# A four-layer convolution and attention kernel: layer 0's middle tap from a moved copy, a rewritten entrance to the attention, and a rewritten end

## The chip, the core and the metric

The kernel runs on one core of one Trainium2 chip. The metric is the time of one execution in device microseconds (us); the runs of the kernel before gave 946.99 to 947.26 us, with a median of 947.2 us. A profiler's record of one execution gives the durations in this document. Its engines are PE (matrix products; PEld is its loading of weights), DVE (the vector engine), ACT (the scalar engine, which evaluates functions), POOL (the general-purpose engine, which also issues some DMAs) and SP (which here only issues DMAs). Each engine works through its own instructions in the order in which they were written to its queue, and waits on semaphores for the others. SBUF is the working memory of 128 partitions; PSUM holds the results of PE in banks of 512 words.

## The reference

Sixteen images of 256 channels and 28 x 28 pixels pass through four layers. Cut to what matters here:

```python
# layer 0: binary activation and binary 3x3 convolution, batch norm over all images, residual
y  = sat_conv2d(sign(x), sign(w0)) * scaling
x  = (y - mean(y)) * rsqrt(var(y) + eps) * gamma + beta + x
# layer 1: sign(x) into a 3x3 convolution with real weights, gates, a 1x1 convolution, batch norms
# layer 2: two binary 3x3 convolutions with batch norm and prelu
out = prelu(binconv(sign(bn(x)), w1), a1)
out = prelu(binconv(sign(bn(out)), w2), a2)
x   = prelu(bn(out) + x, a3)
# layer 3: attention inside each image, N = 784 pixels, 64 channels for q, k and v
q, k, v = Wq @ xf, Wk @ xf, Wv @ xf
attn = softmax(q.T @ k / 8)
x    = Wp @ (attn @ v) + xf
```

A batch norm needs the moments over all sixteen images, so each layer with one ends in a seam: the last image's convolution must be finished before the next layer's first image can be signed.

## The kernel before

The program has a usual form and a careful form; a flag computed on the chip at the end says whether the usual form's result stands. Only the usual form is of interest here. `forward` does layers 0 to 2, `attend_unshifted` the attention, and `leave` its last part, just ahead of the branch on the flag.

**Binary convolutions.** `sign_layer` (line 384) serves layer 0 and both convolutions of layer 2. For each image, `sign_image` has ACT write the signs as 16-bit values into `fpads`, a padded image of 30 x 30 per channel block, two images deep; the products (line 404) read windows of it at column offsets 0, 1 and 2, the three taps of a row. An image of 28 rows takes 36 products of 392 columns. In layer 2, from the image `direct` on, SP also copies the padded image, moved by one element, into `shifted`, and the middle tap reads offset 0 of the copy: its products come after those of the outer taps. Layer 0 has no such copy. After the products ACT takes the upper of two packed results from PSUM (line 420), DVE the lower (line 422), and DVE computes statistics (line 686 in layer 0, 1276 in layer 2). In layer 0 the weights of later layers are prepared beside this, by `steps`: DVE lines 329, 581, 596 and the helper at line 141, which most two-operand steps share. POOL stores each image's integers to `n0d` (line 688). PSUM pairs for the convolutions are three deep.

The order of the instructions on PE, ACT, DVE and SP is written out by hand; that of POOL in layers 0 to 2 is a scheduler's, and in the attention it is by hand too.

**Fillers.** `keep_busy(n)` puts n products on an idle tile into PE's queue, each of 512 columns. One stands near the end of layer 1 (14 products, ahead of the gate's small products), one at the end of layer 2 (35 products, line 506), one in the attention's entrance (8, line 1479).

**The seam into the attention.** `norm("l2c", ..., late=True)` turns the moments into a scale `sg3` (`l2c_r` in the profile) and a shift `bg3` (`l2c_shift`): ACT's square root (line 147), small DVE steps to line 157, then ACT's shift (line 264). For image 0, in halves of 392 pixels, the block k = 1 of the channels gets scale and residual on DVE (line 1642) and the shift on ACT (line 1646); the block k = 0 gets scale and shift on ACT (line 1464) and the residual on DVE (line 1647); then DVE's prelu (line 1649) and the products for queries and keys (`queries_keys`, line 1486). Both halves of the latter hold queries in partitions 0 to 63 and keys in 64 to 127 of the same PSUM bank; three copies, `keys_to` (line 1497) on ACT, `queries` (line 1493) on ACT and `keys_to` on DVE, take them out one after another. An activation at line 1651 loads ACT's table for the exponential ahead of its first use.

**The attention's loop.** Per image: seven chunks of `scores` (line 1509, PSUM tiles "sc", two deep) with ACT's exponential (line 1513); sums of the exponentials in `sum_up`, three on POOL and three on DVE (lines 1521 and 1523), joined in `sum_all` (line 1526); `values` (line 1530), seven chunks into one PSUM bank "av"; `denominators`; the reciprocal (line 1564); the normalizing product (line 1568); and `project` (line 1598, PSUM tile "mi", one deep) with its addition to the image (line 1609). `take_values` (line 1545) is ACT's copy of the values out of PSUM, which `normalize` multiplies. The next image's queries, keys and values (`project_v`, line 1580, `turn_v`, line 1590) stand in between. Images from 2 on are prepared by `finish_a`, where ACT scales and shifts and POOL issues a DMA that adds the residual, and `finish_b`, DVE's prelu (line 1473). In the first turn, image 1 is prepared the same way, with the residual added by DVE (line 1472).

**The end.** For image 15, `doubts_so_far` (five small DVE steps, lines 1618 to 1622) stands between an addition and the reciprocal of image 14. `leave` takes the last denominators by pixel halves, four chunks of values, the flag, the normalization and projection by pixel halves, and three stores on ACT's queue: block 1 in two pixel halves, block 0 whole between them. `usually` is read into a register of every engine, on which each branches after its last instruction.

Of the kernel before, what the change touches and what calls it, by code (L numbers as in the profile page):

```python
# [27 lines left out]
F32 = mybir.dt.float32  # L28
# [62 lines left out]
def forward(ctx: ExitStack, tc: tile.TileContext, d: dict, out: bass.AP, careful: bool):  # L91
# [52 lines left out]
    def rsqrt(name, v, half=None, beside=None):  # L144

        r, t = (const.tile(list(v.shape), F32, name=name + q) for q in ("_r", "_t"))
        A.activation(t, v, AF.Sqrt)
        if beside:
            beside()
# [88 lines left out]
    def norm(name, moments, gamma, beta, sf=None, then=lambda r: None, late=False):  # L238
# [15 lines left out]
        r = rsqrt(name, v, half, (lambda: V.tensor_scalar(less, m, -1.0, None, ALU.mult)) if late else None)  # L254
# [129 lines left out]
    def sign_layer(pads, w, temp, room, sign, post, steps, moments, blocks, together=1, shifted=None, direct=2):  # L384
# [9 lines left out]
        def products(*js):  # L394
            for j in js:
                pss[j] = conv_ps()
            moved = shifted is not None and blocks[js[0]][0] >= direct
# [30 lines left out]
        def sign_image(i):  # L428

            for r0, r1 in ((0, HR + 1), (HR + 1, S)) if i == 0 else ((0, S),):  # L430
                load = sign(i, slice(r0, r1), lambda k: inner(pads[:, i % 2], k, r0, r1))
                if shifted is not None and i >= direct:
                    to, of = (t[:, i % 2].rearrange("p k a b -> p (k a b)") for t in (shifted, pads))
                    nc.sync.dma_start(out=to[:, 0:-1], in_=of[:, 1:])
# [59 lines left out]
    with tc.tile_pool(name="ps_conv", bufs=3, space=PSUM) as psc, \  # L494
# [13 lines left out]
        with tc.tile_pool(name="ph1", bufs=1) as ph:  # L508

            fpads = sign_pads(ph, "vs") if careful else sign_pads(const, None)  # L510
            xs, ns = [None] * B, [None] * B
# [180 lines left out]
            sign_layer(fpads, w0, temp, room0, sign0, post0, steps, mom, whole_images(PARTS), together=2 if careful else 1)  # L692
# [425 lines left out]
            with tc.manual_schedule(engines={ET.PE, ET.DVE, ET.Activation, ET.SP}):  # L1118
# [60 lines left out]
                keep_busy(14)  # L1179
# [33 lines left out]
        with tc.tile_pool(name="ph2", bufs=1) as ph:  # L1213
# [123 lines left out]
            else:  # L1337
                keep_busy(35)
                with tc.manual_schedule(engines={ET.DVE, ET.Activation}):
                    sg3, shift3 = norm("l2c", mom, pv("g3"), pv("b3"), sf2, late=True)  # L1340
                    bg3 = shift3(b3c)
# [78 lines left out]
def attend_unshifted(ctx, tc, d, out, wqk, wv, wp, keys, worst, doubts, flag, pv, finish):  # L1420
# [62 lines left out]
    def queries_keys(b, h, ps):  # L1483

        for k in range(2):
            T.matmul(  # L1486
                ps[:, h, :HN], lhsT=wqk[:, k, :], rhs=x[b][:, k, h * HN:(h + 1) * HN], start=(k == 0), stop=(k == 1)
            )
# [6 lines left out]
    def keys_to(b, rows, h, ps):  # L1495
        copy = A.copy if rows else V.tensor_copy
# [37 lines left out]
    def values(b, c):  # L1534
        if c == 0:
            avs[b] = one_bank(psav, "av")
        side_by_side(avs[b], va[b % 2][:, c, :], es[b, c], c == 0, c == NC_ - 1)
# [98 lines left out]
    with tc.manual_schedule(engines={ET.PE, ET.Activation, ET.DVE, ET.Pool, ET.SP}):  # L1636
# [3 lines left out]
        for n in cuts:  # L1640
            v = x[0][:, 1, n]
            V.scalar_tensor_tensor(v, v, sg3[:, 1:2], x2[0][:, 1, n], ALU.mult, ALU.add)
        for h, n in enumerate(cuts):
            finish_a(0, n, (0,))
            v, w = (x[0][:, k, n] for k in range(2))
            A.activation(w, w, AF.Identity, bias=bg3[:, 1:2])
            V.tensor_tensor(v, v, x2[0][:, 0, n], ALU.add)
            for k, y in enumerate((v, w)):
                V.scalar_tensor_tensor(y, y, alpha[:, k:k + 1], y, ALU.mult, ALU.max)
            queries_keys(0, h, ps[h])  # L1650
        A.activation(ph.tile([P, 2], F32, name="e"), sg3, AF.Exp, scale=0.0)
        keep_busy(8)
        for h in range(2):
            keys_to(0, 1, h, ps[h])
            queries(0, h, ps[h])
            keys_to(0, 0, h, ps[h])
        finish_a(1)
        scores(0, 0)
        project_v(0)
        finish_b(1, ks=(0,))  # L1660
        turn_v(0)
        finish_b(1, ks=(1,))
        V.transpose(ones.rearrange("p a i -> p (a i)"), turned.rearrange("p a i -> p (a i)"))
        for b in range(B - 1):
            scores(b, 1)
            if b > 0:
                take_values(b - 1)
            if b == 0:
                finish_a(2)
            if b > 1:  # L1670
                project(b - 2, 0)()
            sum_up(b, 1)
            scores(b, 2)
# [286 lines left out]
```

## Time and profile before

| what | value |
|---|---|
| median of three runs | 947.2 us |
| the profiled execution's own time | 948.88 us |
| its span, from the first instruction to the last | 947.1 us |
| PE busy | 930.2 us (98%) |
| DVE, ACT, POOL busy | 759.9, 676.1, 139.0 us |
| granted PE clock, mean | 0.996 |
| layer 0 | about 10 to 109 us |
| layer 1 | about 115 to 464 us |
| layer 2 | 464 to 662 us |
| attention | 662 to 940 us, stores and closing to 947 us |

The profile has several views. The chain of waits follows the work that ended last back to the beginning: at each step to what released it, or to the instruction before it on its engine. A piece of it has a start, a length, an engine and the written tile with its line; neighbouring pieces of the same kind are merged with a count. The timeline lists the instructions with start, length, engine, line, operation and tiles, again merged, and in brackets the idle time before. A product in four bytes per word (f32) shows as two records. An engine's busy share is an average over stages with different limits, so each stage is read by itself.

### The profile page before, as it was taken

Reading aid. Unit: us, or ns where it says so; the run is one execution under the profiler, and the core shown is the slowest. Engines: PE = TensorE matmul, PEld = TensorE weight load, DVE = VectorE, ACT = ScalarE, POOL = GpSimd, SP = SyncE. Lnnn points to the kernel's source line nnn. Section 1 sums busy time; section 2 is a strip of 40 time slices with the busy share of each in tenths; the row PEclk is TensorE's granted clock in tenths of the full one; section 3 lists DMA queues with packets and bytes.
Section 4 is the critical chain, followed back from the end, with each engine's and each line's share of the span. In section 5 each row is a group of like instructions: output and inputs, shape, how many; then the busy total and the mean of one; then the engine's idle time right before and its main releaser. Section 6 shows DMA issues by size and latency. Waiting matters only on the chain.

```text
span 947.1 us, 15041 instructions
## 1 busy us (share of the span) xinstructions
PE 930.2 (98%) x5626; PEld 583.6 (62%) x5632; DVE 759.9 (80%) x1446; ACT 676.1 (71%) x1184; POOL 139.0 (15%) x158
## 2 busy tenths in 40 slices
PE   7999999999999999999999999999999999999996
PEld 3555578888788888887555565556444444444442
DVE  3877888999998889987888887889656868777676
ACT  5766578888888788874777767776766666676653
POOL 2001100000000000000000000000235353443422
PEclk9999999999999999999999999999999999999999
DMA  9877533454543344320566201111142433425212
GB/s 334 292 284 272 187 121 122 173 186 177 198 163 139 139 157 163 143 112 35 207 241 214 113 40 60 79 79 59 31 73 70 97 108 81 125 69 136 69 63 112
DMA packets 39733, 130.70 MB, mean 138 GB/s; under 512 B 4882, under 2 KB 16852, under 8 KB 39652
## 3 DMA queue, kind: packets, MB, share of 16 engines
q1 hardware_dynamic: 33332, 98.31, 28.8%
q0 software_dynamic: 5632, 30.54, 11.8%
q8 instruction: 46, 0.75, 0.3%
q10 hardware_dynamic: 688, 0.80, 0.2%
q14 instruction: 35, 0.29, 0.1%
HBM read 72.67 MB, written 32.11 MB: 111 GB/s over the span
## 4 chain that ended last, share of the span: by engine, by line
PE 95%; DVE 2%; ACT 1%; DMA 1%; issue 0%; SPq 0%; DVEq 0%; ACTq 0%
PE cv L404 31%; PE cv L810 29%; PE sc L1509 8%; PE av L1530 8%; PE cv L937 5%; PE mi L1486 5%; PE sm L1580 2%; PE unused L506 2%; PE mi L1598 2%; PE sm L1530 1%; PE gate L905 1%; DMA st<-in_w_dram 1%; PE hid L713 1%; DVE r L1564 1%; DVE p L1609 0%
## 5 line engine op out<-in xcount | busy, mean ns | idle before, releaser
L810 PE MATMUL cv<-vs,w 128*128 128x392 f32 (+1 forms) x1296 | 272.4, 352 | 0.3 <-DVE vs L141 0.3
L404 PE MATMUL cv<-fpads,wpk 128*128 128x392 f16 (+1 forms) x1458 | 249.3, 327 | 2.2 <-DVE wpk L329 1.2
L404 PEld LDWEIGHTS <-wpk 128*128 128x128 f16 x1782 | 172.1, 97 | 123.6 <-issue 4.3
L810 PEld LDWEIGHTS cv<-vs,w 128*128 128x128 f32 x768 | 143.2, 190 | 6.3
L1513 ACT ACTIVATE es<-sc 128x784 f32<-128x784 f32 x112 | 87.4, 823 | 40.0 <-PE sc L1509 40.0
L810 PEld LDWEIGHTS <-w 128*128 128x128 f16 x768 | 69.4, 99 | 51.9 <-issue 9.1
L1509 PE MATMUL sc<-q,keyswa 64*128 64x392 f32 x448 | 89.9, 513 | 1.2 <-ACT es L1513 0.9
L1530 PE MATMUL av<-es,v 128*64 128x392 f32 x448 | 80.7, 499 | 0.0
L1268 DVE SCALAR_TENSOR_TENSOR p<-ab,vec 128x392 f32<-128x392 int16 (+1 forms) x132 | 78.1, 605 | 0.0
L420 ACT ACTIVATE ab<-cv 128x392 int16<-128x392 f32 (+1 forms) x66 | 32.1, 486 | 56.1 <-PE cv L404 53.2
L1523 POOL TENSOR_TENSOR sum<-sum,es 128x784 f32<-128x784 f32 x32 | 67.2, 2101 | 2.5
L1509 PEld LDWEIGHTS sc<-q,keyswa 64*128 64x128 f32 x448 | 38.9, 186 | 44.0 <-issue 17.1
L404 PE MATMUL cv<-shifted,wpk 128*128 128x392 f16 (+1 forms) x324 | 60.6, 322 | 0.0
L810 PE MATMUL cv<-one_on,w 128*128 128x392 bf16 x240 | 59.4, 329 | 0.0
L965 POOL DMA_DIRECT2D x2d<-x x16 | 8.6, 536 | 345.3 <-DVE x L959 285.0
L1497 DVE COPY keyswa<-mi 64x392 f32<-64x392 f32 x31 | 16.3, 564 | 53.2 <-ACT q L1493 53.2
L1530 PEld LDWEIGHTS av<-es,v 128*64 128x64 f32 x448 | 29.4, 136 | 47.0 <-issue 46.6
L422 DVE SCALAR_TENSOR_TENSOR ab<-ab,cv 128x392 int16<-128x392 int16 (+1 forms) x66 | 36.1, 547 | 27.5 <-ACT ab L420 26.6
L792 ACT CAST vs<-vs 128x840 fp32r<-128x840 bf16 x63 | 54.1, 883 | 2.5 <-DVE vs L141 2.3
L937 PE MATMUL cv<-z,fw 128*128 128x392 f32 x256 | 48.9, 342 | 0.1
L937 PEld LDWEIGHTS cv<-z,fw 128*128 128x128 f32 x256 | 46.1, 188 | 0.9 <-ACT z L929 0.9
L1486 PE MATMUL mi<-p,wqk 128*128 128x392 f32 x124 | 45.1, 506 | 0.1
(325 smaller groups left out, 1532.9 us busy)
## 6 DMA issues: line engine op xcount, KB each, us to landing
xs<-in_x_dram SPq DMA_DIRECT2D x30, 784.0 KB, 5.0
one_on<-vs SPq DMA_DIRECT2D x60, 209.8 KB, 2.9
x2d<-x POOLq DMA_DIRECT2D x16, 784.0 KB, 3.6
out_dram<-p SPq DMA_DIRECT2D x15, 784.0 KB, 3.6
shifted<-fpads SPq DMA_DIRECT2D x26, 449.8 KB, 2.8
p<-x2d POOLq DMA_DIRECT2D x14, 784.0 KB, 6.8
p<-x2d SPq DMA_DIRECT2D x13, 784.0 KB, 5.8
n0d<-n POOLq DMA_DIRECT2D x16, 392.0 KB, 4.4
```

What stands on the lines that cost most here:

```text
L404: T.matmul(pss[j][:, n // size if careful else h, :rows * S].rearrange("p (a b) -> p a b", b=S), lhsT=w[:, n, c, :], rhs=src[:, blocks[j][ ...
L420: A.activation(by_halves(ab[:, 1], blocks[j]), ps, AF.Copy, scale=1.0 / PACK)
L422: V.scalar_tensor_tensor(a, b, -PACK, ps, ALU.mult, ALU.add)
L792: copy(v, w)
L810: T.matmul(ps.rearrange("p (a b) -> p a b", b=S), lhsT=w[:, k, c, u, mo * P:(mo + 1) * P], rhs=one_on[:, u, k, :, 0:S] if moved and c == 1 ...
L937: T.matmul(ps[:, h, :HN], lhsT=w[:, k, mo * P:(mo + 1) * P], rhs=z2[b][:, k, h * HN:(h + 1) * HN], start=(k + i == 0), stop=(k + i == 2),)
L1268: V.scalar_tensor_tensor(p, y, alpha[:, mo:mo + 1], y, ALU.mult, ALU.max, accum_out=mom.sums_at(at, mo)[0] if mom.by_sums(at, mo) else None,)
L1486: T.matmul(ps[:, h, :HN], lhsT=wqk[:, k, :], rhs=x[b][:, k, h * HN:(h + 1) * HN], start=(k == 0), stop=(k == 1))
L1509: T.matmul(ps[:, h, :HN], lhsT=chunk[rows], rhs=qs[b][rows], start=True, stop=True)
L1513: A.activation(e, ps[:, :, :HN], AF.Exp, scale=0.125)
L1523: (V if late else nc.gpsimd).tensor_tensor(sums[b, late], sums[b, late], e, ALU.add)
L1530: T.matmul(ps[64 * h:64 * h + 64, :HN], lhsT=w, rhs=e[:, h, :], start=start, stop=stop)
```

## The change

- `sign_layer` gets `until` and `copy`: for images from `direct` up to `until` it makes a moved copy by the given engine. Layer 0 calls it with a tile `moved0`, `until=12` and POOL's `tensor_copy`, so images 2 to 11 read the middle tap from a copy that POOL makes.
- Two fillers are shorter: 14 to 12 in layer 1's end, 35 to 31 before the attention; the one of 8 in the entrance is gone.
- `norm` and `rsqrt` get an activation that loads a table right behind the square root; for `l2c` it is the exponential's. The one in the entrance is gone.
- The entrance is rewritten: both blocks of image 0's first half take scale and residual in one DVE step; the first half's product starts with k = 1; the second half's queries and keys go to two PSUM tiles (`queries_keys_apart`), and both key copies of it are DVE's. `project_v(0)` and `turn_v(0)` come ahead of the first scores. Image 1's second block takes scale and residual on DVE too. Scores 0 to 3, POOL's three sums and values 0 and 1 of image 0 come ahead of image 1's queries and keys, and `finish_a(2)` comes after them.
- `doubts_so_far` moves from image 15 to the loop's turn b = 3.
- Image 14 is normalized from PSUM: no `take_values`, the product reads `av`.
- In `leave`, values run by pixel halves, five chunks each (two chunks stand ahead, not three); the PSUM tiles of the last two projections are swapped; and four stores, one for each block and pixel half, alternate between ACT's queue and SP's.

The diff, without the lines that only shift arguments:

```diff
@@ rsqrt
         A.activation(t, v, AF.Sqrt)
+        if then:
+            A.activation(small.tile(list(v.shape), F32, tag="mv", name="table"), v, then, scale=0.0)
@@ sign_layer
-            moved = shifted is not None and blocks[js[0]][0] >= direct
+            moved = shifted is not None and direct <= blocks[js[0]][0] < until
...
-                if shifted is not None and i >= direct:
+                if shifted is not None and direct <= i < until:
                     to, of = (t[:, i % 2].rearrange("p k a b -> p (k a b)") for t in (shifted, pads))
-                    nc.sync.dma_start(out=to[:, 0:-1], in_=of[:, 1:])
+                    copy(out=to[:, 0:-1], in_=of[:, 1:])
@@ layer 0
+            moved0 = None if careful else ph.tile([P, 2, 2, S + 2, S + 2], SIGNS, tag="vs", name="moved0")
...
-            sign_layer(fpads, w0, temp, room0, sign0, post0, steps, mom, whole_images(PARTS), together=2 if careful else 1)
+            sign_layer(fpads, w0, temp, room0, sign0, post0, steps, mom, whole_images(PARTS), together=2 if careful else 1,
+                       shifted=moved0, until=12, copy=nc.gpsimd.tensor_copy)
@@ layer 1's end
-                keep_busy(14)
+                keep_busy(12)
@@ layer 2's end
-                keep_busy(35)
+                keep_busy(31)
                 with tc.manual_schedule(engines={ET.DVE, ET.Activation}):
-                    sg3, shift3 = norm("l2c", mom, pv("g3"), pv("b3"), sf2, late=True)
+                    sg3, shift3 = norm("l2c", mom, pv("g3"), pv("b3"), sf2, late=True, table=AF.Exp)
@@ attention
+    def queries_keys_apart(b, h, qps, kps):
         for k in range(2):
+            for i, ps in enumerate((qps, kps)):
+                rows = slice(64 * i, 64 * i + 64)
+                T.matmul(
+                    ps[rows, h, :HN], lhsT=wqk[:, k, rows], rhs=x[b][:, k, h * HN:(h + 1) * HN],
+                    start=(k == 0), stop=(k == 1),
+                )
...
-    def values(b, c):
+    def values(b, c, n=slice(0, HN)):
@@ entrance, new
+        for k, n in ((1, one), (0, one), (1, two)):
+            to_x2(0, k, n)
+        for k in (1, 0):
+            shifted(0, k, one)
+            prelu(0, k, one)
+        queries_keys(0, 0, ps[0], (1, 0))
+        finish_a(0, two, (0,))
+        shifted(0, 1, two)
+        add_x2(0, 0, two)
+        for k in range(2):
+            prelu(0, k, two)
+        kps = two_banks(pssc, "sc")
+        queries_keys_apart(0, 1, ps[1], kps)
+        keys_to(0, 1, 0, ps[0])
+        queries(0, 0, ps[0])
+        keys_to(0, 0, 0, ps[0], A.copy)
+        queries(0, 1, ps[1])
+        for rows in range(2):
+            keys_to(0, rows, 1, kps, V.tensor_copy)
+        finish_a(1, ks=(0,))
+        to_x2(1, 1)
+        project_v(0)
+        turn_v(0)
         scores(0, 0)
+        scores(0, 1)
+        shifted(1, 1)
+        add_x2(1, 0)
+        for k in range(2):
+            prelu(1, k)
+        sum_up(0, 1)
+        scores(0, 2)
+        scores(0, 3)
+        sum_up(0, 2, 3)
+        for c in range(2):
+            values(0, c)
+        finish_a(2)
@@ loop
             if b > 0:
                 denominators(b - 1)
+                if b == 3:
+                    doubts_so_far()
                 invert(b - 1)
@@ image 15
-        take_values(b - 1)
+        os[b - 1] = (buf("o", 2, shape=(P, HN)), buf("r", 2, shape=(P, HN)))
...
-        doubts_so_far()
...
-        normalize(b - 1)
+        o, r = os[b - 1]
+        V.tensor_tensor(o, avs[b - 1][:, :HN], r, ALU.mult)
...
-        for c in range(3):
+        for c in range(2):
             values(b, c)
@@ leave
-            for c in range(3, NC_):
-                values(b, c)
+            for n in parts:
+                for c in range(2, NC_):
+                    values(b, c, n)
...
-                adds.append(project(b, mo, two_banks(pssc, "sc") if mo else two_banks(psmi, "mi"), parts[1]))
+                adds.append(project(b, mo, two_banks(psmi, "mi") if mo else two_banks(pssc, "sc"), parts[1]))
...
-            nc.scalar.dma_start(out=by_parts[0], in_=by_parts[1])
-            store(b, slice(0, 1), nc.scalar)
-            nc.scalar.dma_start(out=by_parts[2], in_=by_parts[3])
+            for n in parts:
+                for mo, queue in enumerate((nc.scalar, nc.sync)):
+                    to, of = (halves(t[:, mo, :])[:, :, n] for t in (out[b], x[b]))
+                    queue.dma_start(out=to, in_=of)
```

## The prediction

> **What bounds the kernel now.** I read the page first, then the chain of waits in order of time, then the timeline around each place that the diff touches. The page says that the chain is TensorE nearly throughout, at full granted clock:
>
> ```profile
> PE 95%; DVE 2%; ACT 1%; DMA 1%; issue 0%; SPq 0%; DVEq 0%; ACTq 0%
> ```
>
> So a change pays only where it shortens PE's stream or a seam between stages. The chain's pieces (start, length, what) show both:
>
> ```profile
> 10.46 98.73 PE cv L404 x588
> ...
> 566.25 96.11 PE cv L404 x594
> 662.41 7.51 PE unused L506 x34
> 670.02 1.55 PE mi L1486 x4
> ...
> 674.84 0.93 PE sc L1509 x4
> ...
> 925.02 2.53 DVE r L1564
> ...
> 927.64 1.47 DVE o L1568
> ...
> 934.28 2.66 PE av L1530 x16
> ```
>
> Layer 0 needs 98.73/588 = 167.9 ns per product; layer 2's second convolution, which reads its middle tap from a moved copy, 96.11/594 = 161.8 ns. The starts within one image say why: products of the middle tap follow after 177 ns, the others after 165 to 170. A whole image lasts 6.12 us in layer 0 and 2 x 2.985 = 5.97 us in layer 2. From 662 to 675 the seam is filler, a wait for copies, then attention; from 916 DVE leads.
>
> DVE and POOL exclude each other, as the timelines show (start, length, engine, line):
>
> ```profile
> 743.13 2.05 DVE L1523 TENSOR_TENSOR sum<-sum,es 128x784 f32<-128x784 f32 x1
> ...
> 750.67 0.93 DVE L1521 TENSOR_TENSOR sum<-es 128x784 f32<-128x784 f32 x1
> ...
> 924.89 3.78 POOL L1523 TENSOR_TENSOR sum<-sum,es 128x784 f32<-128x784 f32 x2
> ...
> 927.64 1.46 DVE L1568 TENSOR_TENSOR o<-o,r 128x392 f32<-128x392 f32 x1
> ```
>
> The same addition takes 0.93 alone and 2.05 beside a POOL addition; the product o<-o,r takes 0.57 in other images and 1.46 here. L1609, which adds PSUM to SBUF, keeps 0.97 either way.
>
> **Layer 0's moved copies.** Images 2 to 11: 12 middle-tap products of 36 each get cheaper, 6.12 - 5.98 = 0.14 us per image, **-1.4 us**. The copy of 1799 halfwords runs on POOL. No row shows one: POOL's fill of 448 words took 0.47 (1.05 ns per element, hence 1.9 us), its addition of 784 with two inputs 1.85 (2.36 ns, hence 4.25 us). I take 1.9, since a copy has one input. The copy starts when ACT's signs end, 2.4 us after the preceding image's products begin, and is wanted 6.0 + 24 x 0.166 = 10.0 us after that: 7.6 us of room. POOL's queue also issues n0d (0.54), after DVE's L422; both ends fit in 6.0 us together. Who waits for POOL is DVE's weight work (two SBUF inputs: L141, L596, L329), which follows the statistics at about 3.9 us into the image, so 0.4 us of waiting at 1.9 us per copy. DVE is busy 3.4 to 5.4 us of 6.1 per image there, and three PSUM pairs let L422 lag; hidden. [...] at 4.25 us per copy DVE would wait 2.8 us per image, and still recover between copies. Images 12 to 15 and layer 0's end keep their times.
>
> **Fillers in layer 1's end (14 to 12).** The filler ends at 459.43; the gate's sums are ready at 458.91, but ACT is in its square until 459.50, so ACT's hidden unit moves from 459.79 to 459.52. The square root after the table load also needs DVE's variance (462.15), so it moves from 462.34 to 462.19: **-0.15** (0 to -0.3).
>
> **The attention's entrance.** Exp's table now loads behind the root, at 666.36, before the shifts that ACT began at 667.24. They begin at 667.76, and the first half's entry is shifted at 668.96, not 668.51. Before, the load cost nothing:
>
> ```profile
> 670.02 1.55 PE L1486 MATMUL mi<-p,wqk 128*128 128x392 f32 x4
> 670.16 1.28 ACT L1651 ACT_TABLE_LOAD   x1
> ...
> 671.45 0.20 ACT L1651 ACTIVATE e<-l2c_r 128x2 f32<-128x2 f32 x1
> ...
> 671.67 0.48 ACT L1497 COPY keyswa<-mi 64x392 f32<-64x392 f32 x1
> ```
>
> It ended with PE's products. [...] here the next activation starts at 1.29, so I charge 1.3[...]. Onward with these rows (0.58 per half-image DVE step, 0.51 to 0.61 on ACT): DVE does three entries by 668.97, prelu k=1 at 669.58, k=0 at 670.14. The filler (31 x 0.215) ends at 669.1, no longer in the way; PE's k=1 product starts at 669.65, the half is done at 671.15 (before 671.57). Second half: ACT 670.07 and 670.59, DVE's last prelu 671.81, PE done at 672.83 (673.10). Queries and keys now lie in two PSUM tiles: one ACT copy beside two DVE copies, not three in turn; keys complete at 673.9, while PE does project_v until 674.2. Scores 0 and 1 start there and end by 675.9; before, the same work ended at 678.1. Then ACT's exponentials gate PE: scores 2 and 3 end at 677.5, values 0 and 1 at 678.9.
>
> Next late is image 1's last prelu (L1473, two SBUF inputs). POOL's sums are new here: the first, ready at 676.85, waits for DVE's first prelu (676.5 to 677.5), [...] and the second prelu, ready at 677.6, ends at 680.25. PE's image-1 keys end at 682.4, not 681.8; pv, scores 4 to 6, the remaining values and image 1's first scores (all by their old rows) end at 690.4, against 692.18: **-1.8** (-2.4 without the block; +0.5 if POOL takes two turns). On POOL's queue image 2's accumulating load now stands behind three sums: issued at 684, not 681.1, landing 6.6 later at 690.7; its two prelus end at 692.7 and PE wants them at 693.2 and 693.9. Small cover: later sums go straight onto the path.
>
> **doubts_so_far, moved to b = 3.** Five small DVE steps, 0.95 us from the tail's row. In the steady loop nothing covers them:
>
> ```profile
> 753.52 2.61 DVE L1564 RECIPROCAL r<-sm 128x392 f32<-128x392 f32 x1
> ...
> 756.16 0.57 DVE L1568 TENSOR_TENSOR o<-o,r 128x392 f32<-128x392 f32 x1
> ...
> 756.65 0.97 DVE L1609 TENSOR_TENSOR p<-mi,p 128x784 f32<-128x784 f32 x1
> ...
> 757.76 0.84 PE L1598 MATMUL mi<-o,wp 64*128 64x392 f32 x4
> ```
>
> L1609 frees the only "mi" buffer at 757.62 and PE takes it at 757.76: 0.1 of slack, so **+0.85** once.
>
> **The tail.** Without the doubts the reciprocal of image 14 starts when the denominators are there, 924.2 (925.0 before). Normalizing from PSUM escapes POOL: 0.57, done at 927.4 (929.1), and ACT's copy goes. PE then waits for score banks (ACT until 928.5): projections 928.15 to 929.5, two values to 930.9, then DVE's last sum, ready 931.3 (POOL holds it until 928.7). Denominators end at 932.95 (the bank must be freed at 932.25), against 934.28. Values by pixel halves: 40 records of 196 columns at 0.083 (L1558's 8 took 0.66), end 936.3 against 936.94, the first half at 934.6. DVE's reciprocals end at 935.8, o's at 936.75, and with the two PSUM tiles swapped only the fourth addition waits: the last ends at 939.05, not 940.34: -1.3.
>
> The stores: same bytes, four of 784-byte rows. Before, the last was issued at 940.37, landed at 945.37, and 1.7 us of closing followed[...]. Now the last issue is near 939.1, moving done by 941.0, landing 941.6 to 943.2. But SP branches only after its last store: the trace has 2.5 us from SP's branch to its next instruction, 4.2 for ACT and DVE. SP resumes at 942.1 to 943.8, passes nine semaphores (0.7), then 1.65 of closing: the span ends at 944.4 to 946.1, not 947.1: **-1.0 to -2.7, taken -1.8**.
>
> **Sum.** -1.4 - 0.15 - 1.8 + 0.85 - 1.8 = -4.3. The profiled execution took 948.88 (span 947.1 and 1.8 around it) and would take 944.6; the runs' median is 947.2 and would be **943.0**.
>
> **Rivals.**
> - *The entrance is eaten by POOL's sums*: [...] image 2's load lands after 693. For it: the rows above[...]. Entrance +0.3 instead of -1.8: 945.1.
> - *POOL bounds layer 0 (slower)*: if a copy costs X, each image costs X + 0.54 instead of 6.12. From X = 5.9 us on it outweighs all other gains (2.9); at 7 us it is 10 x 1.42 = +14.2, so 958.5. Against: the two-input row gives only 4.25.
> - *The middle tap doesn't follow the copy* (layer 2 differs in something else): no 1.4, 944.4. The start-to-start times speak against.
> - *The tail gives more*: [...] entrance unblocked: 941.3.
>
> **Chances.** Forecast 0.58 (own range 941.8 to 944.4), entrance eaten 0.17, no tap gain 0.08, better tail 0.10, POOL-bound 0.07. A measurement tells 0.2% (1.9 us, so 945.3 and 949.1). Faster takes all but the slow rival and some of the eaten entrance: 0.80; same 0.12; slower 0.08. The range leaves out the slow rival and a little at each end: 940.9 to 946.3.
>
> **What would show it.** "moved" products 165 ns apart, POOL copies near 1.9 us; the filler before attention ending before the first product; ACT's table load at 666.4 less the earlier gains; a DVE L1473 of about 2 us near image 1; one loop turn (b = 3) 0.85 longer; o<-av,r at 0.57; the last store issued 1.3 earlier relative to image 15's scores. Wrong if POOL's copies exceed 5 us, if image 2 arrives late, or if the closing is set by fetches alone.

## The result, and the profile after

The changed kernel takes 944.72 us (median of ten runs, 944.31 to 946.44); the kernel before, run beside it, 947.2 us. The ratio is 0.9974, with a 95% interval from 0.9965 to 0.9982: faster by 2.5 us, where the forecast was 4.2 us, 943.0. The range (940.9 to 946.3) holds the time; the forecast's own narrower range (941.8 to 944.4) misses it by 0.3 us.

The page of the kernel after begins with these lines. POOL has 19 us more work, DVE 5 us more, PE about 5 us less than the 930.2 of before (3.3 less than the 928.7 of a second profile of before):

```profile
span 943.0 us, 15081 instructions
...
PE 925.4 (98%) x5637; PEld 582.3 (62%) x5642; DVE 764.7 (81%) x1446; ACT 675.4 (72%) x1183; POOL 158.1 (17%) x168
```

The chain of waits is empty for this execution, so the timelines have to serve. In layer 0 they now show, per image, 24 products of the outer taps and 12 of the moved copy, 5.98 us apart from image to image (38.21 to 44.19), where it was 6.12. Each copy takes POOL 1.70 us (one 1.83), and all but one stand right behind a store, whose issue mostly waits for DVE:

```profile
38.21 2.16 PE L406 MATMUL cv<-moved,wpk 128*128 128x392 f16 x12
40.20 4.15 PE L406 MATMUL cv<-fpads,wpk 128*128 128x392 f16 x24
44.19 2.16 PE L406 MATMUL cv<-moved,wpk 128*128 128x392 f16 x12
...
44.99 0.54 POOL L691 DMA_DIRECT2D n0d<-n  x1 [4.09 <-DVE n L424]
45.53 1.70 POOL L436 COPY moved<-fpads 128x1799 f16<-128x1799 f16 x1
```

In the entrance, the table for the exponential is loaded early, and the next activation starts 1.29 us after the load began. PE's first product waits for DVE's prelu. Image 1's two prelus (L1671) and POOL's first sum hold each other up: 3.61 us for two steps. PE (L1490, second piece) waits for the later of them:

```profile
663.75 1.28 ACT L149 ACT_TABLE_LOAD   x1
665.04 0.20 ACT L149 ACTIVATE table<-l2c_v 128x2 f32<-128x2 f32 x1
...
667.26 1.55 PE L1490 MATMUL mi<-p,wqk 128*128 128x392 f32 x4 [0.83 <-DVE p L1671]
...
674.19 3.61 DVE L1671 SCALAR_TENSOR_TENSOR p<-p,vec 128x784 f32<-128x784 f32 x2
...
674.45 2.52 POOL L1536 TENSOR_TENSOR sum<-es 128x784 f32<-128x784 f32 x1 [11.55 <-ACT es L1528]
...
677.86 2.24 PE L1490 MATMUL mi<-p,wqk 128*128 128x392 f32 x6 [0.18 <-DVE p L1671]
```

At the end, PE's values by halves end at 933.24, both products o follow together, and part 1's first projection (the second "sc" line) starts only when the second addition is done:

```profile
929.75 3.49 PE L1553 MATMUL av<-es,v 128*64 128x196 f32 x40
...
933.29 0.63 DVE L1815 TENSOR_TENSOR o<-av,r 128x196 f32<-128x196 f32 x2 [0.87 <-PE av L1553]
...
934.14 0.50 PE L1617 MATMUL sc<-o,wp 64*128 64x196 f32 x4
...
934.84 0.55 DVE L1628 TENSOR_TENSOR p<-sc,p 128x392 f32<-128x392 f32 x1
...
935.45 0.60 PE L1617 MATMUL sc<-o,wp 64*128 64x196 f32 x4 [0.81 <-DVE p L1628]
...
936.58 0.55 DVE L1628 TENSOR_TENSOR p<-mi,p 128x392 f32<-128x392 f32 x1
```

Where the time went can be read from marks that both traces have: the same product or the same addition in each. The span fell by 4.05 us between the two profiled executions, more than the medians differ, and layer 0's last product alone came 2.40 us earlier. The first experiment settles that.

### The profile page after: what moved, and what is told of

Read it like the earlier page. It is cut to its first block, busy times and chain, and to the rows that moved or that the text cites. A ratio compares the mean times of both kernels' runs of the same rounds, so it can differ in the third digit from the quotient of the medians.

```text
span 943.0 us, 15081 instructions
## 1 busy us (share of the span) xinstructions
PE 925.4 (98%) x5637; PEld 582.3 (62%) x5642; DVE 764.7 (81%) x1446; ACT 675.4 (72%) x1183; POOL 158.1 (17%) x168
## 4 chain that ended last, share of the span: by engine, by line
## 5 line engine op out<-in xcount | busy, mean ns | idle before, releaser
L406 PE MATMUL cv<-fpads,wpk 128*128 128x392 f16 (+1 forms) x1338 | 228.3, 325 | 2.3 <-DVE wpk L331 1.3
L1553 PE MATMUL av<-es,v 128*64 128x392 f32 (+1 forms) x468 | 81.0, 485 | 0.0
L1536 POOL TENSOR_TENSOR sum<-es 128x784 f32<-128x784 f32 x16 | 31.1, 1941 | 101.5 <-ACT es L1528 91.4
```

Source lines behind the costliest of these rows:

```text
L406: T.matmul(pss[j][:, n // size if careful else h, :rows * S].rearrange("p (a b) -> p a b", b=S), lhsT=w[:, n, c, :], rhs=src[:, blocks[j][ ...
L1536: (V if late else nc.gpsimd).tensor_tensor(sums[b, late], es[b, c - 1], e, ALU.add)
L1553: T.matmul(avs[b][64 * h:64 * h + 64, n], lhsT=va[b % 2][:, c, :], rhs=es[b, c][:, h, n], start=(c == 0), stop=(c == NC_ - 1 and n.stop == ...
```

## The experiments

In all of them "the changed kernel" is the one after, and stage times are distances between two marks in one trace.

**A second profile of the kernel before.** No edit.

> The kernel before, unchanged, for a second profile. Between the two profiles layer 0's last product came 2.40 us earlier after the change, where ten cheaper images explain 1.36 (the sum over the images, 10 x about 0.136). Theory: the other 1.0 belongs to the execution, since in the first profile of before TensorE's granted clock was 0.5 to 0.6 between 10 and 14 us, and the first image took 7.77 us. Then a second profile of before has its first image near 6.5 us and a span about 1 to 1.7 us shorter (945.4 to 946.1). Rival: the change itself shortened the start; then the first image takes 7.8 us again and the span is 947.1 again.

Span 945.24 us, run 947.02 us. The 36 products from layer 0's seventh on take 6.52 us, where the first profile has 7.77 (the expectation calls them the first image; they reach six products into the second). They differ in the clock that PE was granted. The rows by stretch of time (first the first profile, then the second; the clock stands behind the busy times of the five engines):

```profile
10.00:12.00 2.00, 1.54 (x5) 0.71 (x6) 1.10 (x3) 1.72 (x3) 0.00 (x0) 0.63 1.03 405
12.00:14.00 2.00, 2.00 (x8) 0.92 (x7) 1.14 (x3) 1.65 (x2) 0.00 (x0) 0.51 1.09 412
```

```profile
10.00:12.00 2.00, 2.00 (x13) 0.99 (x13) 1.11 (x2) 1.73 (x3) 0.00 (x0) 1.00 1.04 409
12.00:14.00 2.00, 2.00 (x13) 1.15 (x13) 1.11 (x2) 1.10 (x2) 0.00 (x0) 1.00 1.09 403
```

So about 1 us of the first comparison belonged to the execution. The common mark from here on is layer 0's 54th product, in the middle of the second image. In the fourteen profiles of this study it comes between 18.3 and 20.1 us: in five of them (19.8 to 20.1) PE had half the clock for 3.4 us from 10.2 to 10.6 us on, in the other nine (18.3 to 19.0) it had the full clock there. From that product on, before has 926.99 and 926.93 us in its two profiles and the changed kernel 924.02: **-2.9 us**, which the following table divides. It uses the second profile.

| stage, by marks | before | after | difference |
|---|---|---|---|
| layer 0: the 54th product to the last product | 88.82 | 87.51 | -1.31 |
| layer 1's end to layer 2's first product (fillers) | 8.16 | 8.01 | -0.15 |
| layer 2's last product to image 2's `project_v` (entrance) | 35.61 | 34.23 | -1.38 |
| image 4's `project_v` to image 5's (the turn b = 3) | 16.41 | 17.27 | +0.86 |
| image 15's `project_v` to DVE's last addition | 29.98 | 29.95 | -0.03 |
| DVE's last addition to the end of the span (closing) | 6.82 | 5.91 | -0.91 |
| all else | | | +0.01 |

**Layer 0's copies undone.**

```diff
-                       shifted=moved0, until=12, copy=nc.gpsimd.tensor_copy)
+                       )
```

> The changed kernel with layer 0's moved copies undone, all else as changed. Theory: products back at a repeating 165, 177, 166 ns, images 2 to 11 at 6.12 us, layer 0's products 1.36 us longer from the second image on, the total +1.4 us (about 946.1 where the changed kernel has 944.7), POOL's busy time back from 158 to about 139 us. Rival 'the copies give 2.4': +2.4. Rival 'the middle tap doesn't follow the copy': +0.

945.99 us; ratio to before 0.9988 (0.9981 to 0.9995), so the copies are worth 1.27 us by the medians. The trace has 6.12 us per image again and 88.83 us in the first row of the table: 1.32. The products follow the copy, and the copy gives what ten images should give; the rival that it gave 2.4 falls.

**Two copies per image, and four.**

```diff
-                    copy(out=to[:, 0:-1], in_=of[:, 1:])
+                    for _ in range(2 if until < B else 1):
+                        copy(out=to[:, 0:-1], in_=of[:, 1:])
```

> The changed kernel with each of layer 0's POOL copies made twice (same data into the same place). POOL's time per copy was 1.9 us, now 3.8, plus 0.54 for the store it issues: 4.3 of 5.98 us per image. Theory (the copy has 7.6 us of room and DVE's waits recover within an image): images 2 to 11 keep 5.98 us and the total changes by less than 0.3 us. Rival [...]: DVE's weight work waits 1.9 us longer per image and images grow to over 6.1 us, +1 to +6 us.

> Each POOL copy made four times: 4 x 1.9 + 0.54 = 8.1 us of POOL per image against 5.98 us of TensorE. Theory: POOL sets the pace of layer 0 from about 5.4 us of copying on, so images 2 to 11 take about 8.1 us and the total is 10 x 2.15 = +21 us, less what the buffers let run ahead (4 to 8 us). Rival 'nothing waits for the copies': images stay at 5.98 us. This shows where the slow rival of the forecast would have begun.

948.70 us with two (ratio 1.0016, 1.0010 to 1.0023) and 978.3 us with four (one run). Both expectations are missed: 3.5 us of copying and a store's 0.54 fit well into 5.98 us, and yet layer 0 grew by 3.64 us; with four, the span grew by 33.4 us, where POOL's throughput explains about 14 (4 x 1.70 + 0.54 = 7.34 us per image instead of 5.98). In the trace with four the middle-tap products wait 25.2 us in all for their copies. After the three longest waits (7.75, 6.40 and 3.04 us) the granted clock stood at half, 0.50 between 37.5 and 44.3 us for one, and 12 products took 3.6 to 3.8 us instead of 2.16; that makes 4.6 us more:

```profile
41.00 3.77 PE L406 MATMUL cv<-moved,wpk 128*128 128x392 f16 x12 [7.75 <-POOL moved L437]
```

The trace with two shows images of up to 6.91 us, and PE waiting for the copies:

```profile
38.66 2.16 PE L406 MATMUL cv<-moved,wpk 128*128 128x392 f16 x12 [0.53 <-POOL moved L437]
...
45.58 2.16 PE L406 MATMUL cv<-moved,wpk 128*128 128x392 f16 x12 [0.77 <-POOL moved L437]
```

The copies before the second of these start 5.5 us after ACT's last sign (36.50), because the store ahead of them in POOL's queue waits for DVE; and DVE is late, since the copies before held it (L585 takes 2.04 us here and 0.55 at the same place of the changed kernel). ACT in turn waits for DVE's L585. POOL's, DVE's and ACT's timelines of the kernel with two copies:

```profile
41.45 0.54 POOL L692 DMA_DIRECT2D n0d<-n  x1 [2.85 <-DVE n L424]
41.99 3.54 POOL L437 COPY moved<-fpads 128x1799 f16<-128x1799 f16 x2
```

```profile
36.98 2.04 DVE L585 TENSOR_SCALAR st<-st 128x768 f32<-128x768 f32 x1
```

```profile
39.05 0.42 ACT L596 ACTIVATE w<-st 128x256 f16<-128x256 f32 x1 [2.55 <-DVE st L585]
```

**Two copies, with the store on SP's queue.**

```diff
-                    nc.gpsimd.dma_start(out=n0d[b], in_=ns[b])
+                    nc.sync.dma_start(out=n0d[b], in_=ns[b])
```

> As the run with two POOL copies per image, but the store of n0 is issued on SP's queue instead of POOL's. In that run the copies stood in POOL's queue behind that store, which waits for DVE's difference L424 of the image before, and six of ten first middle-tap products waited 0.2 to 0.8 us for their copy. Theory [...]: the copies now start when ACT's signs end, end 2 to 3 us earlier, no product waits for them, images 2 to 11 return to 5.98 to 6.05 us (layer 0 about 3 us shorter than with two copies on POOL's queue). Rival [...]: DVE's weight work is still blocked, ACT's signs come late behind it, and layer 0 keeps at least 2 of the 3.4 us.

All copies but two now start 0.06 us after the signs; the two stand 0.5 us behind the preceding image's copies. Layer 0 takes 88.67 us, where it was 91.15 with two copies on POOL's queue and is 87.51 with one: of the 3.64 us lost, 2.5 were the queue. The other 1.2 lie at one place: image 6's middle-tap products start 7.14 us after image 5's, all others up to image 11 5.98 to 5.99. PE waits there for ACT's signs; ACT had waited 2.96 us for DVE's L585, which takes 2.03 us beside the copies:

```profile
37.70 2.03 DVE L585 TENSOR_SCALAR st<-st 128x768 f32<-128x768 f32 x1
39.77 0.42 ACT L596 ACTIVATE w<-st 128x256 f16<-128x256 f32 x1 [2.96 <-DVE st L585]
46.40 4.24 PE L406 MATMUL cv<-fpads,wpk 128*128 128x392 f16 x24 [0.74 <-ACT fpads L530]
```

The run as a whole, 947.3 us (one run), keeps little of that: layer 1's first product comes 1.9 us later behind layer 0's last one than in the changed kernel. SP's queue also loads what layer 1 begins with, so the stores ahead of these loads are a likely cause; it was not followed up.

**The old entrance in the changed kernel.** The block from the first `to_x2` to the loop is replaced by that of before, with 35 and 8 fillers and the table load behind the first products.

> The changed kernel with the attention's entrance of before: its order of steps, one two-bank tile per half for queries and keys together, Exp's table behind the first products, 35 fillers, POOL's three sums of image 0 after the queries and keys of image 1. Theory (the forecast's step, as the traces sized it): the third projection of values (image 2), counted from layer 2's last product, comes 1.37 us later than in the changed kernel; the total is +1.4 (about 946.1). The forecast's own size was +1.8. Rival 'the entrance is eaten by POOL's sums': +0 or a gain.

946.05 us (ratio to before 0.9988, 0.9981 to 0.9995): +1.33 by the medians; the entrance takes 35.60 us, +1.37.

**POOL's first sums behind image 2's load.**

```diff
-        sum_up(0, 1)
         scores(0, 2)
         scores(0, 3)
-        sum_up(0, 2, 3)
         for c in range(2):
             values(0, c)
         finish_a(2)
+        sum_up(0, 1)
+        sum_up(0, 2, 3)
```

> The changed kernel with POOL's three sums of image 0 moved in POOL's queue behind the accumulating load of image 2[...]. Theory ([...] the difference of -1.8 and -2.4 in the forecast): the two preludes take 2.0 us, image 1's queries and keys end about 1.5 us earlier than in the changed kernel, ACT's exponentials then gate, and the third projection of values comes 0.6 us (0.3 to 1.0) earlier; image 2's load is issued at about 678.5 instead of 681.4. Rival: ACT's exponentials gate there anyway and the block costs nothing: 0.0. Rival: the sums now meet a later DVE step and it is 0.5 us slower.

944.27 us (ratio to before 0.9967, 0.9953 to 0.9980), and an entrance of 33.72 us, 0.51 less than the changed kernel's. The prelus take 2.08 us for two, and the queries and keys of image 1 run in one piece:

```profile
673.94 2.08 DVE L1671 SCALAR_TENSOR_TENSOR p<-p,vec 128x784 f32<-128x784 f32 x2
...
676.50 2.90 PE L1490 MATMUL mi<-p,wqk 128*128 128x392 f32 x8
```

They end 0.46 us earlier, not 1.5: PE has values to do until 676.50, so it becomes the bound as soon as DVE is no longer late. The gain, 0.5, is close to the 0.6 that the forecast put on the block; the run also issues image 2's load earlier, for which PE had not waited.

**doubts_so_far in DVE's idle time.**

```diff
                 sum_up(b - 1, 6)
+                if b == 3:
+                    doubts_so_far()
...
                 denominators(b - 1)
-                if b == 3:
-                    doubts_so_far()
```

> The changed kernel with doubts_so_far, in the same turn b = 3, put behind sum_up(b - 1, 6), ahead of DVE's idle time of 3.1 to 3.7 us before it copies keys, instead of ahead of the reciprocal. Theory (the five small steps cost 0.85 only because nothing covers them where they are): projections of values 4 to 5 lie 16.41 us apart as in the other turns, not 17.27; everything from image 5 on and the span 0.85 us earlier. Rival: the steps cost what they take wherever they stand (0.95): no change.

The turn takes 16.41 us again, and the one run 943.74 us. Here one of the five steps even meets a POOL addition (L1640, 1.21 us, where it took 0.16), and DVE still has 1.19 us of idle time left before its next step:

```profile
724.84 1.21 DVE L1640 SCALAR_TENSOR_TENSOR sure<-some,sure 128x1 f32<-128x1 f32 x1
726.09 0.15 DVE L1641 TENSOR_SCALAR worst<-sure 128x1 f32<-128x1 f32 x1
727.43 1.05 DVE L1512 COPY keyswa<-mi 64x392 f32<-64x392 f32 x2 [1.19 <-ACT q L1508]
```

**The stores of before.**

```diff
-            for n in parts:
-                for mo, queue in enumerate((nc.scalar, nc.sync)):
...
+            nc.scalar.dma_start(out=by_parts[0], in_=by_parts[1])
+            store(b, slice(0, 1), nc.scalar)
+            nc.scalar.dma_start(out=by_parts[2], in_=by_parts[3])
```

> The changed kernel with its last stores as before: three on ACT's queue (half of channel block 1, the whole of block 0, the other half of block 1) instead of four on two queues. Nothing before the last addition changes. In the profile the closing after DVE's last addition took 6.75 us before (and 6.83 in the second profile of before) and 5.91 after the change. Theory: the four stores are what shortened it, so this kernel is +0.85 us, with the last store landing about 5.0 us behind its issue instead of 2.75. Rival: the closing is set by instruction fetches after the branch[...]: +0 within 0.2.

944.30 us (943.99 to 945.96, ratio to before 0.9969, 0.9956 to 0.9981) and a closing of 5.76 us: the four stores on two queues bought nothing. In the trace with three, SP branches early and waits for the stores, and the span ends 1.72 us after the last one has landed; so it does in both profiles of before. But that store lands 4.0 us after its issue here, and 5.0 and 5.1 us after it there. With four, SP branches 0.53 us after the last addition (937.66 in the changed kernel) and goes on 3.13 us later (940.79), when all has landed, and the span ends 2.25 us after that; the last distance is the same in ten of the eleven traces with four stores (2.41 with four copies). The two ways cost the same here. The profile's list of issues shows the large store before that last one landing 3.9 us after its issue in this kernel and 4.9 us in the second profile of before:

```profile
out_dram<-p ACTq DMA_DIRECT2D x1, 392.0 KB, 3.9
```

```profile
out_dram<-p ACTq DMA_DIRECT2D x1, 392.0 KB, 4.9
```

So with four stores the closing is 0.53 us, SP's time from its branch to its next instruction, and 2.25 us; only the middle term varies. In most traces it goes with the start of PE's last fetch of instructions (the queue with packets of 16 KB is taken for PE's, which has most instructions), but two and four copies don't fit:

| kernel | fetch after the last addition | SP, branch to next | closing |
|---|---|---|---|
| doubts in idle time / two copies, store on SP / changed kernel / old entrance | 0.12 to 0.14 | 3.31 / 3.20 / 3.13 / 3.26 | 6.09 / 5.98 / 5.91 / 6.04 |
| two copies / four copies | 0.21 / 0.26 | 3.53 / 3.66 | 6.31 / 6.59 |
| copies undone / sums later | 0.57 / 0.59 | 3.44 / 3.33 | 6.22 / 6.11 |
| combined (below) | 0.83 | 3.64 | 6.42 |
| second combined (below) | 1.11 | 3.90 | 6.68 |
| tail (below) | 1.33 | 3.91 | 6.70 |
| stores of before (three) | 0.44 | not the limit | 5.76 |
| before, two profiles (three) | 1.56, 1.44 | not the limit | 6.75, 6.82 |

That the fetch causes it is not shown, and neither is what sets its start, nor why the last of three stores lands earlier in one kernel than in the other. With the stores of before in the changed kernel the fetch starts 1.1 and 1.0 us earlier than in the two profiles of before (0.44 us after the last addition, for 1.56 and 1.44), and the last store lands 1.0 and 1.1 us sooner after its issue (4.0 for 5.0 and 5.1); no run isolates the one from the other.

**The last image's tiles.** Part 1's first projection goes into `last`, and the values run over whole rows again.

```diff
-                adds.append(project(b, mo, two_banks(psmi, "mi") if mo else two_banks(pssc, "sc"), parts[1]))
+                adds.append(project(b, mo, two_banks(psmi, "mi") if mo else last, parts[1]))
...
-            for n in parts:
-                for c in range(2, NC_):
-                    values(b, c, n)
+            for c in range(2, NC_):
+                values(b, c)
```

> The changed kernel with two edits in the last image's end: part 1's first projection goes into the tile `last` (its flag has been read by then) instead of a new "sc" tile, and chunks 2 to 6 of the values are taken over all columns again, not by pixel halves. Theory: both products o (L1815) waited for the last value in the changed kernel, so the halves bought nothing and the values end at the same time (20 records of 392 columns for 40 of 196); the new "sc" tile shares its two banks with part 0's second projection and waited for the second addition, `last` does not: counted from the last value's end, DVE's last addition comes 0.75 us earlier than in the changed kernel (its last value product starts at 932.91, its last addition ends at 937.13: 4.22; expected 3.5). Rival: part 1's projections wait for something else (o, or the first addition): 4.2 or 3.8.

From the start of these values to the last addition's end 6.56 us, where the changed kernel has 7.38: -0.82. All eight records of part 0's second and part 1's first projection run through, and the values take the same time in 20 records as in 40:

```profile
930.72 3.46 PE L1553 MATMUL av<-es,v 128*64 128x392 f32 x20
...
935.08 0.83 PE L1617 MATMUL sc<-o,wp 64*128 64x196 f32 x8
...
936.72 0.56 DVE L1628 TENSOR_TENSOR p<-mi,p 128x392 f32<-128x392 f32 x1
```

The one run took 945.85 us all the same: its closing is 6.70 us, 0.79 more than the changed kernel's, and its start was a late one (the 54th product at 19.79), with the clock at half.

**What the runs point to, together.** Copies for images 2 to 15, POOL's sums later, the doubts in idle time, and a last image whose values lie by halves in two tiles (only a part of the last one's edit is shown):

```diff
+        mi = two_banks(psmi, "mi")
+        halves_av = [one_bank(psav, "av")[:, 0:HN // 2], mi[:, 0, 0:HN // 2]]
...
+            y = two_banks(pssc, "sc")
+            adds = [project(b, 0, y, parts[0]), project(b, 1, last, parts[0]), project(b, 0, mi, parts[1])]
+            adds[0]()
+            adds.append(project(b, 1, y, parts[1]))
```

> The changed kernel with what the runs point to together: layer 0's copies for images 2 to 15 (4 x 0.136 = -0.55 more), POOL's first three sums behind image 2's load (-0.5), doubts_so_far in DVE's idle time (-0.86), and a last image whose values lie by halves in two tiles ("av" and the first bank of "mi"), each with its reciprocal and product as soon as its half is there, and whose four projections use "sc", `last`, "mi" and "sc" again (-1.2). Sum -3.1: 941.6 where the changed kernel has 944.7. Rival: the last images' copies meet POOL's sums of the doubts (L230 to L233) at layer 0's end, or the tail waits elsewhere: 942.5 to 943.5.

945.36 us (ratio to before 0.9982, 0.9975 to 0.9989), so no better than the changed kernel. The first three parts gave what they should (0.55, 0.51 and 0.86), and the end lost 1.65 us: ACT's sums over the denominators had come behind both of DVE's reciprocals, the flag's product waits for ACT, and the projections stand behind it in PE's queue:

```profile
931.20 0.33 ACT L1824 ACTIVATE junk<-sc 128x196 f32<-128x196 f32 x1 [6.95 <-DVE r L1818]
...
933.55 0.19 PE L1646 MATMUL sc<-turned,w 128*1 128x1 f32 x2 [2.52 <-ACT junk L1645]
933.67 0.93 PE L1617 MATMUL sc<-o,wp 64*128 64x196 f32 x8
```

With ACT's sums back between the reciprocals, and both reciprocals ahead of both o:

> As the run 'combined', with the order of the last image's end mended: there ACT's sums over the denominators (L1824) stood behind both reciprocals, the flag's product waited 2.52 us for them on TensorE, and all four projections stood behind it. Now they stand between the reciprocals as in the changed kernel, and both reciprocals ahead of both products o. Theory: the flag's product follows the last value at once, projections start about 0.2 us behind it and no addition waits for another's bank; from the start of chunk 2's values (L1553 at 929.75 in the changed kernel, last addition's end 937.13: 7.38) to the last addition's end 6.2 us; the closing stays between 5.8 and 6.8 us behind it, as in all runs so far. With -0.55, -0.5 and -0.86, which 'combined' showed at their places, the total is 1.9 + 1.2 = 3.1 us below the changed kernel's 944.7, at a closing like its own: 941.6, and 942.4 at the long closing. Rival: the tail waits elsewhere again, or a closing of its own takes it back: 942.8 and more.

942.72 us (ratio to before 0.9959, 0.9943 to 0.9974), the fastest here, 2.0 us below the changed kernel by the medians, 1.7 by the distances to the kernel before run beside each; with six runs its interval still overlaps the changed kernel's (0.9965 to 0.9982). From chunk 2's values to the last addition it takes 6.17 us (7.38), and the first o no longer waits for the last value:

```profile
930.57 0.30 DVE L1825 TENSOR_TENSOR o<-av,r 128x196 f32<-128x196 f32 x1
931.53 0.36 DVE L1825 TENSOR_TENSOR o<-mi,r 128x196 f32<-128x196 f32 x1 [0.66 <-PE mi L1796]
...
933.61 0.56 DVE L1628 TENSOR_TENSOR p<-sc,p 128x392 f32<-128x392 f32 x1
```

It missed 941.6 by two items: the closing, 6.68 us, took 0.77 back, and the seam between layers 0 and 1 was 0.57 us longer than in the changed kernel (6.80 for 6.23), which no run explains; in the first combination, with the same copies, it was 6.32.

## Why the prediction was right or wrong

**Layer 0: right in size, its room misjudged.** -1.4 forecast, -1.31 measured, and the copy took 1.70 us where 1.9 was taken. Wrong was the margin. The step gave the copy "7.6 us of room" by the signs' end; by the trace the ten copies end 2.9 to 5.6 us before they are wanted. The signs end 2.5 to 5.0 us after the preceding image's first product for images 3 to 11, not 2.4, which leaves 5.0 to 7.5 us, and the copy starts up to 2.5 us behind them, since it stands in POOL's queue behind a store that waits for DVE. And the rival "POOL bounds layer 0" was put at "From X = 5.9 us on it outweighs all other gains (2.9)", by POOL's throughput alone. At two copies of 1.7 us, 3.5 together, layer 0 already lost 3.6 us. Two copies made the kernel slower than before (948.70), so the upper bound of the copy's cost, 4.25 us, at which the forecast estimated that DVE would "still recover between copies", would have done so too, as far as one long copy acts like two. The right side was reached by the value chosen, not by the margin argued.

**The fillers: right.** -0.15 forecast and measured.

**The entrance: right in mechanism, too large.** -1.8 forecast, -1.38 measured. The steps came in the order and nearly at the times that were worked out: with the shift of 2.62 us that layer 2's last product shows, the first product was due at 667.03 and came at 667.26, the second half was to be done at 670.21 (670.36), the second prelu at 677.63 (677.80), image 1's keys at 679.78 (680.03), and its second scores at 687.78 (688.12). Each step is 0.15 to 0.35 late; nothing new came in. The table load was charged at 1.3 by the row of before, and again the next activation started 1.29 us after the load began. POOL's block was priced at 0.6 and gave 0.51 when it was taken away; the two prelus took 3.61 us beside POOL and 2.08 alone, as the forecast's rows had one addition at 2.05 beside POOL and at 0.93 alone. The rival "entrance eaten" didn't happen: DVE waited 3.02 us for image 2's load, which landed at 688.04 (forecast, with the shift: 688.08), and PE didn't wait for it.

**doubts_so_far: right.** +0.85 forecast, +0.86 measured, and gone where DVE has idle time.

**The tail: wrong.** -1.8 forecast for additions and closing, -0.94 measured. The first steps hold: the product o<-av,r took 0.56 and the denominators ended at 929.92, which is where 932.95 falls with the shift of 3.18 that image 15 shows, but for 0.15 us. Two steps failed after that.
- "Values by pixel halves" was to have the first half ready early. Both products o waited for the last value, as one row of two with one wait shows. The values of both halves lie in one PSUM tile, and PE raises its count for them once, with their last product. This step had been credited with little, since DVE's reciprocals ended late, but it is the reason that nothing overlapped.
- "with the two PSUM tiles swapped only the fourth addition waits: the last ends at 939.05, not 940.34: -1.3". Against that the last addition came 0.03 us earlier. In the built program `last` lies in PSUM banks 0 and 1, and the new "sc" tile does not take them over, though the flag has been read; it lies in banks 2 and 3, as part 0's second projection does, and so PE waits for the second addition, 0.47 us later than it would for the first one. Using `last` itself gave 0.82. By the forecast, with the shift, the last addition was due at 935.87 and came at 937.13: of the 1.26 us, 0.35 are the later o, and the tile accounts for 0.8.

**The closing: right for four stores, wrong in what it was compared with.** By the sum, 0.5 of the -1.8 was left for it, and it gave 0.91. SP's late branch, its 2.5 to 4.2 us to the next instruction (3.13 measured) and the 0.7 and 1.65 us behind it (2.25) were foreseen, and they are what ends the span. But the stores of before close as fast at this place, since their last one lands a microsecond sooner there than in the kernel before. So the gain is not the four stores', and its cause stays open.

**The sum.** The forecast's terms add up to -4.3, so 942.9 rather than 943.0. The misses are 0.9 in the tail, 0.4 in the entrance and 0.1 in layer 0. The parts as measured make -2.9; the medians make -2.5. The gap of 0.4 is not traced. It may lie in the closing, which took 5.9 to 6.6 us in the eight traces with the same end, the changed kernel's own being the shortest; or ahead of the 54th product, which at the full clock came at 18.3 us in the one such trace of before and at 18.3 to 19.0 in the eight others. Single executions start up to 1.8 us apart, which is why the first pair of profiles said 4.05. By its number alone the result, 944.72, lies nearer to two rivals (944.4 without the tap's gain, 945.1 with the entrance eaten) than to the forecast; only the marks inside the traces, and the runs without the copies and with the old entrance, tell that neither of them happened.

## What to carry to other kernels

Room for a moved step is counted from where its own queue lets it start, not from when its data is ready: whatever stands ahead of it, and whatever that waits for, comes off the margin (up to 2.5 us here), and doubling the step once on the chip shows whether the margin is there (here it cost 3.6 us). A tile that the source has finished with need not be free (a projection waited 0.47 us longer here), and a result split into halves was split only where each half had its own tile and its own signal (the first o at 930.57 in the second combination, ahead of the last value; both behind it in the changed kernel); look up the banks and the wait before counting on an overlap. Compare stages by marks inside each trace: two single spans of the kernel before differ by 1.9 us (947.1 and 945.24), more than any one stage changed.

## What the runs showed of the hardware

- PE's granted clock at the start differs from execution to execution with the same program: 0.63 and 0.51 between 10 and 14 us in one profile of before, 1.00 in the other. Layer 0's 54th product then comes at 20.10 or 18.31 us. The two rows lack 0.37 x 2 + 0.49 x 2 = 1.7 us of full clock, which is half speed for 3.4 us. Five of the fourteen traces have such a stretch of 3.4 us at half at the start.
- A second copy of 1.7 us ran on POOL, which had 3.7 us free per image, and made layer 0 3.6 us longer over ten images: it delayed DVE (L585 2.04 us instead of 0.55), DVE delayed the store's issue and ACT, and these delayed the next copies. With the store on another queue 1.2 us were left.
- After the branch at the end, ACT needed 3.0 to 3.9 us to its next instruction, DVE 3.4 to 4.2 and SP 3.1 to 3.9 in the eleven traces with four stores; POOL needed 0.43 us in all but one of them.
